# Attention and perception in one kernel: a quarter of the attention products as three passes of exact parts, dx and guides by eight products, taps along whole padded rows

## The chip, the cores and the metric

The kernel runs on one core of a Trainium2 chip. A core has a matrix engine (TensorE, in the profile PE, with its weight loads listed as PEld), a vector engine (VectorE, DVE), an activation engine (ScalarE, ACT), a general engine (GpSimd, POOL) and SyncE (SP), which here only issues DMAs. Each engine works through its own queue in order, and waits on semaphores for the others. Matrix products go from SBUF into PSUM, which has eight banks of 512 fp32 columns. The metric is the device time of one execution in microseconds, the median of the runs. The kernel before takes 3396.79 us (three runs, 3394.53 to 3397.17).

## The reference

Two layers work on a tensor of 4 images of 64 x 64 pixels with 256 channels, in fp32.

Layer 0 is full self-attention over the 4096 pixels of an image:

```python
q = x @ Wq + bq
k = x @ Wk + bk
v = x @ Wv + bv
energy = jnp.einsum('bnd,bmd->bnm', q, k)      # d = 32
attn = jax.nn.softmax(energy, axis=-1)
x_out = jnp.einsum('bnm,bmc->bnc', attn, v)
out = gamma * x_out.reshape(B, H, W, Cin) + inputs
```

Layer 1 takes its result: a depthwise 3 x 3 convolution with three outputs per channel ("perceived", 768 channels), a 1 x 1 layer to 512 channels with an exact gelu ("hidden"), a 1 x 1 layer back to 256 channels (dx) which is added to the pixels, and then an attention of each pixel over its 3 x 3 neighbours:

```python
scores = stack([(q * kp[:, 1+dy:1+dy+Hh, 1+dx:1+dx+Ww, :]).sum(-1) for dy, dx in _POS]) * scale
w = softmax(scores, axis=-1)
out = sum of w[..., i:i+1] * vp[:, 1+dy:1+dy+Hh, 1+dx:1+dx+Ww, :]
```

## The kernel before

Channels lie on partitions. The 16384 pixels are taken in 32 blocks of 512 (eight rows), eight to an image, and the program walks through 32 slots. In slot s the attention of block s is computed, the convolution of block s - 2 (`perceive`), and hidden layer, dx, guide and scores of block s - 3 (`k`), and the local products of block s - 5 (`a`). Everything is written out in order by hand, so a queue's order is the program's.

A slot has 16 points, one for each half group of 256 keys (`G`, `half`). At a point the program issues, in this order: loads for later groups; the energies (a matmul of keys and queries in the single-pass fp32 form, `float32r`) and the exponentials of them on ACT (`weight`) for two points ahead; the point's jobs (`jobs[point]`); the half group's product (`product`, L352: weights times values into two accumulators); the sum of the next half group's weights on DVE (`add_up`, L366); and then so many DVE steps of the convolution as `share` says for this point (L1152). A step is one tap (L505: window times a weight, added to the accumulator) or one of four mixes per output triple (L511). The first tap of an output is done by ACT (L501).

Ordinary fp32 matmuls appear as two instructions, those in `float32r` form as one.

The hidden layer uses Strassen's scheme in Winograd's form, seven half-size products and additions for eight products (`hidden_part`, L610 and L617). So do dx (`update_part`, with `seven`, `gather` and `update_mix`) and guides (`guide_part`, `guide_mix`): guides stand for q and k of the local attention in one, h times Wq Wk'. Their products are collected by DVE additions (L574, L576) and a few ACT copies.

At the end of a slot DVE folds the weights' sums and sums them over 32 x 32 squares (`partial_sums`, L386 and L387), a small matmul adds them over partitions (dps, L405), DVE inverts the result and spreads it (`finish`, L408, L394, L397), multiplies the accumulators by it (L417) and adds them to the pixels in the ring `xp` (L423). PE's order is: dps, then energies and point 0's jobs of the next slot, then its first product, which needs the accumulators free.

POOL works on the local attention's masks (L989) and denominators (`local_sum`, L1012). In slots 7, 15 and 23 the next image's projections of q, k and v are made as well, two or three at every second point (`projections`), and kept in DRAM; keys and values come back from there by DMAs on SP's queue (`load_keys`, `load_values`).

## Time and profile before

| | |
|---|---|
| median of 3 runs | 3396.79 us |
| profiled execution, its own time | 3395.35 us |
| its span | 3393.6 us |
| PE busy, products L352 | 3364.7 us (99%), 1833.3 us |
| DVE busy, taps L505 | 2747.1 us (81%), 1108.1 us |
| ACT busy | 1074.8 us (32%) |
| POOL busy | 352.1 us (10%) |
| DMA | 285 MB, 84 GB/s |
| granted clock of PE | 0.998 |

The busy time of an engine is the union of its instructions; the page's groups give, after the count, the busy time in us and the mean time of one in ns, and the idle time in front of them. Matmuls overlap, so the time that a series of them needs is read from the starts, not from the single durations. The page's slices show DVE at eight tenths from slot 2 on, with hardly a change from slot to slot; most slots take 99.5 us, the first ones less, and those with projections 136 us. In the views of one stretch each line has start and duration in us, engine, line, operation, the tiles (written <- read) and the number of instructions merged, and in brackets the idle time before and what ended it.

### The profile page before, as it was taken

Reading aid. Unit: us, or ns where it says so; the run is one execution under the profiler, and the core shown is the slowest. Engines: PE = TensorE matmul, PEld = TensorE weight load, DVE = VectorE, ACT = ScalarE, POOL = GpSimd, SP = SyncE. Lnnn points to the kernel's source line nnn. Section 1 sums busy time; section 2 is a strip of 40 time slices with the busy share of each in tenths; the row PEclk is TensorE's granted clock in tenths of the full one; section 3 lists DMA queues with packets and bytes.
Section 4 is the critical chain, followed back from the end, with each engine's and each line's share of the span. In section 5 each row is a group of like instructions: output and inputs, shape, how many; then the busy total and the mean of one; then the engine's idle time right before and its main releaser. Section 6 shows DMA issues by size and latency. Waiting matters only on the chain.

```text
span 3393.6 us, 32830 instructions
## 1 busy us (share of the span) xinstructions
PE 3364.7 (99%) x11678; PEld 2118.8 (62%) x11678; DVE 2747.1 (81%) x4455; ACT 1074.8 (32%) x1344; POOL 352.1 (10%) x550
## 2 busy tenths in 40 slices
PE   8999999999999999999999999999999999999998
PEld 5556666666666666666666666666666666666655
DVE  2388888867888888876888888887688888988895
ACT  2233333333332333332333323333333333333331
POOL 3000011100111110110001111101110011110031
PEclk9999999999999999999999999999999999999999
DMA  5332222342222222234222222223422222222200
GB/s 170 104 104 65 73 77 78 97 133 89 77 77 81 82 75 71 77 102 140 77 78 78 75 82 83 67 79 107 141 80 68 78 77 70 87 84 66 71 13 26
DMA packets 166126, 285.17 MB, mean 84 GB/s; under 512 B 67284, under 2 KB 68196, under 8 KB 165828
## 3 DMA queue, kind: packets, MB, share of 16 engines
q1 hardware_dynamic: 155684, 263.36, 25.1%
q10 hardware_dynamic: 9696, 17.11, 1.3%
q0 software_dynamic: 576, 2.53, 0.2%
q8 instruction: 95, 1.56, 0.2%
q14 instruction: 75, 0.61, 0.1%
HBM read 240.23 MB, written 41.94 MB: 83 GB/s over the span
## 4 chain that ended last, share of the span: by engine, by line
PE 90%; DVE 7%; DMA 2%; SPq 0%; issue 0%; ACT 0%; ACTq 0%; DVEq 0%; POOL 0%
PE acc L352 47%; PE e L333 7%; PE hid_bc L610 5%; PE hid_de L610 4%; PE hid_gf L610 4%; PE lv L923 3%; DVE perc L505 3%; PE lo L1057 3%; PE v L303 2%; PE hid_a L610 2%; DMA ka<-packed 2%; PE s L964 2%; PE dx_cd L562 1%; PE dx_ab L562 1%; PE dx_eg L562 1%; DVE den L366 1%
## 5 line engine op out<-in xcount | busy, mean ns | idle before, releaser
L352 PE MATMUL acc<-p,v 128*128 128x512 f32 x4096 | 1833.3, 593 | 0.6 <-DVE o L417 0.6
L352 PEld LDWEIGHTS acc<-p,v 128*128 128x128 f32 x4096 | 770.4, 190 | 794.7 <-issue 775.4
L505 DVE SCALAR_TENSOR_TENSOR perc<-xp,wperc,perc 128x512 f32<-128x512 f32 (+2 forms) x1554 | 1108.1, 775 | 27.6 <-ACT perc L501 27.5
L341 ACT ACTIVATE p<-e 128x1024 f32<-128x1024 f32 x512 | 524.8, 1025 | 1676.9 <-PE e L333 758.3
L366 DVE TENSOR_TENSOR den<-den,p 128x1024 f32<-128x1024 f32 x480 | 585.3, 1219 | 74.0 <-ACT p L341 72.2
L333 PE MATMUL e<-qa,ka 128*128 128x512 f32 x1024 | 364.9, 478 | 14.9 <-DMA ka<-packed 8.1
L989 POOL TENSOR_TENSOR lp<-lp,near 128x396 f32<-128x396 f32 x60 | 89.1, 1486 | 2427.8 <-ACT lp L984 2427.8
L333 PEld LDWEIGHTS e<-qa,ka 128*128 128x128 f32 x1024 | 190.5, 190 | 143.8 <-issue 101.8
L610 PE MATMUL hid_de<-perc,wmix 128*128 128x256 f32 x720 | 165.2, 379 | 0.0
L610 PEld LDWEIGHTS hid_de<-perc,wmix 128*128 128x128 f32 x720 | 136.8, 190 | 43.7 <-issue 21.5
L511 DVE TENSOR_TENSOR perc<-perc 128x256 f32<-128x256 f32 x360 | 149.9, 430 | 8.2
L633 ACT ACTIVATE hid<-hid,bup 128x512 f32<-128x512 f32 x120 | 80.4, 717 | 220.0 <-DVE hid L617 220.0
L501 ACT ACTIVATE perc<-xp,bperc,wperc 128x512 f32<-128x512 f32 x192 | 145.9, 809 | 1.7 <-DVE xp L423 1.7
L1012 POOL TENSOR_TENSOR lsum<-lsum,lp 128x99 f32<-128x99 f32 (+1 forms) x179 | 123.7, 698 | 11.7
L923 PE MATMUL lv<-wlv,h 128*128 128x256 f32 x520 | 122.4, 379 | 0.0
L303 PE MATMUL v<-wv,xc 128*128 128x256 f32 x512 | 117.9, 383 | 0.6 <-DMA wv<-in_w_v 0.5
L303 PEld LDWEIGHTS v<-wv,xc 128*128 128x128 f32 x512 | 98.1, 192 | 28.7 <-issue 15.4
L1057 PEld LDWEIGHTS lo<-lp,lv 128*128 128x128 f32 x732 | 104.9, 191 | 17.5 <-issue 9.8
L923 PEld LDWEIGHTS lv<-wlv,h 128*128 128x128 f32 x520 | 98.7, 190 | 15.5 <-issue 2.2
L1057 PE MATMUL lo<-lp,lv 128*128 128x99 f32 (+1 forms) x732 | 104.7, 291 | 0.0
L617 DVE TENSOR_TENSOR hid<-hid_bc,hid 128x512 f32<-128x512 f32 x60 | 41.5, 692 | 75.4 <-PE hid_bc L610 75.4
L341 ACT ACT_TABLE_LOAD x60 | 77.0, 1283 | 76.2 <-PE e L333 75.0
(205 smaller groups left out, 3128.6 us busy)
## 6 DMA issues: line engine op xcount, KB each, us to landing
v<-packed_v SPq DMA_DIRECT2D x248, 512.0 KB
ka<-packed SPq DMA_DIRECT2D x508, 128.0 KB
xp<-in_x SPq DMA_DIRECT2D x30, 528.0 KB
xc<-in_x SPq DMA_DIRECT2D x56, 256.0 KB
out<-lo SPq DMA_DIRECT2D x56, 256.0 KB
packed_v<-vs ACTq DMA_DIRECT2D x48, 256.0 KB
packed<-st SPq DMA_DIRECT2D x16, 512.0 KB
qa<-packed SPq DMA_DIRECT2D x62, 128.0 KB
```

The source lines that it names most:

```text
L303: nc.tensor.matmul(ps[:, i * C : (i + 1) * C], lhsT=xc[:, kin, bass.ts(2 * pair + i, P)], rhs=wv[:, kin, :], start=(kin == 0), stop=(kin = ...
L333: nc.tensor.matmul(e[:, j, :], lhsT=key[:, bass.ts(j, P)].bitcast(F32R), rhs=queries[s].bitcast(F32R), start=True, stop=True,)
L341: nc.scalar.activation(p, energies[s, G][:, 2 * half : 2 * half + 2, :], AF.Exp)
L352: nc.tensor.matmul(accs[s][c], lhsT=v[:, 2 * half + i, bass.ts(c, P)], rhs=p[:, i, :], start=(first and i == 0), stop=(G == NG - 1 and hal ...
L366: nc.vector.tensor_tensor(den, den, p, ALU.add)
L501: nc.scalar.activation(acc, win, AF.Identity, bias=bperc[:, half, j : j + 1], scale=wt)
L505: nc.vector.scalar_tensor_tensor(acc, win, wt, acc, ALU.mult, ALU.add)
L511: nc.vector.tensor_tensor(t[:, to, :], t[:, a, :], t[:, b, :], op)
L610: nc.tensor.matmul(ps[:, n * C : (n + 1) * C], lhsT=w(j), rhs=mixes[s, j][:, kind, :], start=(j == 0), stop=(j == MULT - 1),)
L923: nc.tensor.matmul(ps[:, half * C : (half + 1) * C], lhsT=keys_of(s, t, half, kin), rhs=wlv[:, kin, :], start=(kin == 0), stop=(kin == CH ...
L1012: nc.gpsimd.tensor_tensor(to, to, near_ws[block, half][:, t_, of, :], ALU.add)
L1057: nc.tensor.matmul(pv[:, rows, columns(half)], lhsT=lvs[block, t, half][:, bass.ts(c, P)], rhs=near_ws[block, half][:, t, of, :], start=(i ...
```

## The change

- In slots 1 to 30 four of the 16 half groups (2, 6, 10 and 14: `IN_PARTS`) are no longer multiplied as fp32. ACT makes a rounded "high" part of the weights (`ph`) right after the exponential, DVE a difference `low` and a combination `gap` = high - 4096 low in `add_up`, one point ahead of their use. The values have been split in the same way when they were projected, and lie in DRAM as three forms (`packed_f`). `product` then makes three passes in the single-pass form: values' high part times high, second form times low (into the same accumulators), third times gap into two further accumulators. `finish` scales these on ACT and adds them on DVE.
- The other values are stored scaled by 4096/4097, and gamma carries the inverse.
- Energies are made for one half group at a time, two banks instead of four; the accumulators take four banks instead of two. Keys have two buffers instead of three. The forms are loaded three points ahead (`load_forms`).
- dx and guides use `update` and `guide` (which the last slots used already): eight full products, two banks each, instead of seven of half the width; `seven`, `gather`, `update_mix`, `update_part`, `guide_mix`, `guide_part` and the mixed weights are gone. The jobs move over the points accordingly.
- For blocks up to 29 a tap runs over the padded rows as one run of 8 x 66 - 2 = 526 elements, instead of 8 windows of 64. The mixes take 262 elements for 256, and the hidden layer's products read 64 of every 66 columns.
- `share` has the same sum of 60 steps, laid over the points in another way.

```diff
+SPLIT = 4096.0
+BELOW = 1.0 - 2.0**-13
+IN_PARTS = (2, 6, 10, 14)
...
+            split = 2 * (s % NBLK) + pair in IN_PARTS
+            if not split or s < NBLK or s >= NSLOT - NBLK:
...
+                nc.scalar.activation(v, of, AF.Identity, scale=SPLIT / (SPLIT + 1.0))
...
+            if split:
+                whole, high, low = (fresh(f"v{n}_{s}_{pair}") for n in "whl")
+                nc.scalar.copy(whole, of)
+                nc.scalar.activation(high.bitcast(F32R), of, AF.Identity, scale=BELOW)
+                nc.vector.tensor_tensor(low, whole, high, ALU.subtract)
+                gap = fresh(f"vg_{s}_{pair}")
+                nc.vector.scalar_tensor_tensor(gap, low, -SPLIT, high, ALU.mult, ALU.add)
+                nc.scalar.mul(low, low, SPLIT)
+                for i, part in enumerate((high, low, gap)):
+                    nc.scalar.dma_start(
+                        out=packed_f[:, 2 * s + pair, i], in_=part.rearrange("p t c -> p (t c)")
+                    )
...
-            e = epsum.tile([P, GRP, NB], F32, tag="e", name=f"e_{s}_{G}", bufs=1)
+            e = epsum.tile([P, 2, NB], F32, tag="e", name=f"e_{s}_{G}_{half}", bufs=1)
...
+            if in_parts(s, G, half):
+                high = tile_of([P, 2, NB], "late", f"ph_{s}_{G}_{half}", 4)
+                nc.scalar.activation(high.bitcast(F32R), p, AF.Identity, scale=BELOW)
+                highs[s, G, half] = high
...
+            for part, (w, to, x) in enumerate((
+                (v, 0, highs[s, G, half]), (f[:, :2], 0, lows[s, G, half]), (f[:, 2:], CH, gaps[s, G, half])
+            )):
+                for i in range(2):
+                    for c in range(CH):
+                        nc.tensor.matmul(
+                            accs[s][to + c], lhsT=w[:, i, bass.ts(c, P)].bitcast(F32R),
+                            rhs=x[:, i, :].bitcast(F32R),
...
             nc.vector.tensor_tensor(den, den, p, ALU.add)
+            if in_parts(s, G, half):
+                high = highs[s, G, half]
+                low, gap = (tile_of([P, 2, NB], "late", f"p{n}_{s}_{G}_{half}", 4) for n in "lg")
+                nc.vector.tensor_tensor(low.bitcast(F32R), p, high, ALU.subtract)
+                nc.vector.scalar_tensor_tensor(
+                    gap.bitcast(F32R), low, -SPLIT, high, ALU.mult, ALU.add
+                )
...
+            for o, gap in zip(os, acc[CH:]):
+                nc.scalar.mul(o, gap, -1.0 / (SPLIT + 1.0))
...
+                    if 0 < s < NSLOT - 1:
+                        nc.vector.tensor_tensor(o, acc[c], o, ALU.add)
...
+                if s < NSLOT - LAG_PERC:
+                    acc = percs[s][i][:, :RUN]
+                    win = xp[:, half, bass.ds((at + dy) * WP + dx, RUN)]
...
-                job(local_product, a, 0), job(local_product, a, 1) + job(update_mix, k),
-                job(update_part, k, "ab"), job(update_part, k, "cd") + job(update_part, k, "eg"),
-                job(update_part, k, "f"),
-                job(guide_part, k, "ab") + job(local_values, k, 0) + job(guide_part, k, "cd"),
-                job(guide_part, k, "eg") + job(guide_part, k, "f"), job(scores, k, 0),
-                job(scores, k, 1) + job(local_sum, k - 1), job(border_terms, k), job(border, k), [],
+                job(local_product, a, 0), job(local_product, a, 1),
+                job(update, k, 0), job(update, k, 1), job(guide, k, 0),
+                job(guide, k, 1), job(local_values, k, 0), job(scores, k, 0),
+                job(scores, k, 1) + job(local_sum, k - 1), [], job(border, k), [],
...
-            share = [6, 7, 7, 5, 4, 3, 3, 3, 2, 2, 4, 5, 5, 4, 0, 0]
+            share = [0, 0, 6, 5, 5, 0, 5, 4, 4, 2, 7, 7, 7, 3, 5, 0]
...
+                soon = slot + (point + 3) // points, *divmod((point + 3) % points, 2)
+                if in_parts(*soon):
+                    load_forms(*soon)
```

## The prediction

> **What bounds the kernel now.** I read the page's engine line and chain first, then the stretch of one ordinary slot, then the vector queue at the end of that slot.

> ```profile
> PE 3364.7 (99%) x11678; PEld 2118.8 (62%) x11678; DVE 2747.1 (81%) x4455; ACT 1074.8 (32%) x1344; POOL 352.1 (10%) x550
> ...
> PE 90%; DVE 7%; DMA 2%; SPq 0%; issue 0%; ACT 0%; ACTq 0%; DVEq 0%; POOL 0%
> ```

> The stretch (window, its length, then busy time and count of PE, PEld, DVE, ACT and POOL, granted clock, DMA share, GB/s), and DVE's timeline at its end:

> ```profile
> 1713.00:1813.00 100.00, 100.00 (x350) 63.70 (x350) 86.91 (x141) 31.71 (x39) 10.12 (x15) 1.00 0.24 77
> ```

> ```profile
> 1789.81 2.73 DVE L505 SCALAR_TENSOR_TENSOR perc<-xp,wperc,perc 128x512 f32<-128x512 f32 x4
> 1792.46 1.22 DVE L366 TENSOR_TENSOR den<-den,p 128x1024 f32<-128x1024 f32 x1
> 1793.59 4.09 DVE L505 SCALAR_TENSOR_TENSOR perc<-xp,wperc,perc 128x512 f32<-128x512 f32 x5
> 1797.61 1.21 DVE L366 TENSOR_TENSOR den<-den,p 128x1024 f32<-128x1024 f32 x1
> 1798.74 4.63 DVE L505 SCALAR_TENSOR_TENSOR perc<-xp,wperc,perc 128x512 f32<-128x512 f32 x5
> 1803.30 0.34 DVE L895 TENSOR_SCALAR edge<-h,small 128x8 f32<-128x8 f32 x1
> ...
> 1805.80 1.71 DVE L511 TENSOR_TENSOR perc<-perc 128x256 f32<-128x256 f32 x4
> 1807.42 1.22 DVE L366 TENSOR_TENSOR den<-den,p 128x1024 f32<-128x1024 f32 x1
> 1808.68 0.69 DVE L368 TENSOR_TENSOR den<-den 128x512 f32<-128x512 f32 x1
> 1809.40 0.71 DVE L386 STREAM_TRANSPOSE turned<-den 128x512 f32<-128x512 f32 x1
> ...
> 1811.49 0.69 DVE L387 TENSOR_REDUCE parts<-turned 128x16 f32<-128x512 f32 x1
> 1812.94 0.36 DVE L408 RECIPROCAL inverse<-dps 128x32 f32<-128x32 f32 x1 [0.77 <-PE dps L405]
> ```

> TensorE (PE) bounds it: 99% busy, 90% of the chain. But a slot of 99.5 us holds 86.9 us of VectorE (DVE) work, and at its end both meet: the sums of the weights end at 1812.18, and the small matmul dps that needs them runs at 1812.6, when the last product is through. DVE has half a microsecond in hand there, and its other idle time (some 12 us) lies earlier, where it waits for products. So I add up each engine's queue from one dps to the next; the program's order says what stands where.

> Start-to-start prices from these lines: a tap (L505) 0.663 (2.65/4) when GpSimd (POOL) is idle, 0.80 and 0.91 when it works beside; adding up the weights of a half group 1.13, 1.26 before a dependent one; a mix of taps (L511) 0.41; the fold 0.72; the four passes of the sums 2.78.

> **The change on PE.** A plain product is two instructions per matmul (4096 in the page for 2048), spaced 0.429: 8 make 3.43 us per half group. An energy, already in the single-pass form, is one instruction; four took 0.93 (from the end of a product at 1731.90 to 1732.83). Three passes of four such matmuls cost between 12 x 0.190 (the weight load's row) and 12 x 0.2325: 2.3 to 2.8; I take 2.7, since little of the 0.93 can be a switch. That removes 0.73, four times a slot: -2.9. dx becomes 8 x 2 instructions of half the former count and twice their width: 16 x 0.429 = 6.86 for 28 x 0.216 = 6.05; the guides 8 x 0.429 = 3.43 for 14 x 0.216 = 3.02: +1.2. Energies by pairs may pay a switch twice: 0.465 to 0.50 a pair, taken 0.48, +0.2 a slot. Strided right sides of 64 in 66 columns: no row; 0, as the reads of guides in 32s cost 0.216 like the rest. PE alone would need 98.0 for 99.5.

> **The change on DVE.** Gone with the seven-product forms: 22 additions and mixes of a slot, 10.5 us by their rows (L574 4.1, L576 2.0, L697 to L716 2.8, L834 and L861 1.6). Added: in four points of 16 a difference (as L366: 1.22 with a dependent behind it) and a scale-and-subtract of 1024 elements (no row; L1070, 512 elements with a constant, takes 0.69 as the plain add does, so 1.14, bounds 1.13 and 1.3): 9.4; two additions in finish, 1.4. Each tap has 526 elements for 512: by the step from 448 to 512 elements (0.596 to 0.662) that is +0.014: 0.678, 0.7 a slot. What whole rows may save is the slowdown beside POOL: of 33 taps wholly under the masks' POOL multiply (L989) the median took 1.44 us for 0.747, while 28 contiguous adds (L366) took 1.22, as ever; but ten contiguous mixes under L1012 took 0.585 for 0.425. The bounds are 0 and all of the present 2.7 a slot; L366 is the nearest, being long and contiguous, and I take 0.5. In sum DVE's work hardly grows.

> What decides is where it stands. The new `share` puts no taps in points 0, 1 and 5, where DVE now idles behind PE, and 29 of 60 steps in points 10 to 14, where PE is shortest. Behind the local values of point 10, for which DVE must wait, the queue is: their two adds 0.76; four weight sums 4.52 and one of 1.26; difference and gap of point 14, 2.36; 21 taps 14.2; 8 mixes 3.3; fold 0.72; sums 2.78: 29.9 us. PE in the same stretch: products 2.7, 3.43, 3.43, 3.43, 2.7, 3.43, five pairs of energies 2.4, two scores 2.8, the border 0.1: 24.5. Its dps then waits 5 to 6 us (part of it already in point 14, whose low pass waits for DVE's difference).

> The slot: points 0 to 5 took 46.6 (dps 1713.10 to the energies of point 6 at 1759.66); pairs +0.1, point 2's product -0.7: 45.9. Points 6 to 9: 0.48 each, dx 2 x 3.43, guides 2 x 1.72, products 2.7 and 3 x 3.43; point 10 to its local values 0.48 + 1.73: 27.4. Then 0.27 handing over (1718.13 to 1718.40 for hid_bc), 29.9, and 0.34 to the next dps: **103.8 against 99.5, +4.3**, and 0.5 beside POOL.

> PE's wait has a price of its own, in these three rows (columns as above):

> ```profile
> 50.00:53.50 3.50, 3.50 (x17) 2.81 (x15) 0.00 (x0) 0.59 (x1) 0.00 (x0) 1.00 0.17 61
> 53.50:57.00 3.50, 1.18 (x4) 0.94 (x4) 0.00 (x0) 0.59 (x1) 0.00 (x0) 0.87 0.44 168
> 57.00:60.00 3.00, 3.00 (x6) 1.54 (x6) 1.11 (x1) 1.02 (x1) 0.00 (x0) 0.59 0.13 51
> ```

> After 2.3 us without a matmul the clock was granted at 0.59 over 3 us: about 1.7 us of work lost. A wait of 5 us every slot can bring that each time, or fall with the low clock inside itself. Bounds 0 and 3.4 (two such stretches); I take half of 1.7, 0.85, as some of it passes in the wait. [...]

> **The sum**, against the profiled execution (3395.35 us with a span of 3393.6; the median of the runs is 1.4 more). 23 full slots (5, 6, 8 to 14, 16 to 22, 24 to 30) x 5.65: +130. Slot 4 the same, +6. Slot 3, without local products, +4. Slot 2 is nothing but taps beside products: DVE 37.4 taps and mixes + 18.5 weight sums + 9.4 + 1.4 sums + 5.9 finish + 0.9 round trip = 73.5 for 66.3, and the clock: +8. Slot 1, no taps: 4 x -0.73 and pairs: -2.5. Slots 7, 15, 23, 136 us with the next image's projections, have PE enough to hide DVE: -1.5 each by PE, and about as much back for ACT, which now waits inside a projection for two DVE operations: 0. Slot 0, the same splits, +2. Slot 31 and the tail keep their work: 0. Together +148; **3395 + 148 + 1 = 3544 us**.

> Hidden and costed at nothing: the 64 MB of forms (120 loads of 512 KB on SP's queue, at a 25% DMA share; each issued three points, 10 us or more, ahead, waiting for a product already past; keys queue behind them, with three points of lead too); ACT's 4.3 us of high parts and 1.2 of scaled gaps in a 32% engine. If a key came late, PE would wait as it did for 8.1 us in all on ka. The accumulators are free 4 us after dps (two chained additions more than before), while PE has 6 us of hidden layer and values first.

> **Rivals.**
> - *Taps at contiguous speed* (ends faster). If 526 elements in a row ran at 0.45 or less, the 21 taps would give back 4.8 us, the tail would fit under PE, and each slot would be PE's 98.0: 25 x -1.5, slots 7, 15, 23 -4.5, slots 1 and 2 -5, +2: 3350. Against it: L576, all contiguous with a per-partition scalar, takes 0.39 to 0.40 for 256, as L726 on strided rows does. 0.12.
> - *POOL slows whole rows as it did windows*: 2.2 more in 24 slots, 3597. The mixes' 0.585 speak for it, L366 against. 0.20. [...]
> - *ACT held by the splits*: 16 splits, each holding the exponentials for 5 us (DVE's queue, then a write of the buffer reused): up to +64 on mine, 3608. ACT idles two thirds, the weights are two points ahead. 0.07.

> **How the numbers follow.** Mine 0.58, centre 3544; its own range 3490 (differences 1.13, pairs 0.465, no clock and no POOL loss: +3.2 a slot) to 3610 (gap 1.3, clock 1.7). With the rivals on the slow side 0.85; 0.12 for faster; the rest, 0.03, split. The range 3450 to 3620 leaves out the fast rival and the ends. A change under 0.2%, about what the runs' spread of 0.08% lets one tell, would need the tail to shrink by just 4.5 us: 0.02.

> **What would show it.** Right: DVE over 88 us busy in a slot of about 104 to 106; PE's share falling to 94-96%; waits of PE on DVE parts (dps) of 3 to 5 us in some 25 slots, and of the low pass in point 14; a granted clock under 1 after them; taps at 0.76 each by duration, also beside POOL. Wrong: taps under 0.55, or dps idle under 1 us, or the longest waits in slots 7, 15 and 23.

## The result: slower, and by twice as much as forecast

The changed kernel takes 3695.31 us (median of four runs, 3688.88 to 3705.93), the kernel before 3395.66 (four runs, 3392.83 to 3397.17): a ratio of 1.0887, with a 95% interval of 1.0856 to 1.0917. The forecast was slower, with 0.85, at 3544 us; its range ended at 3620. The sign was right, the size was not: +300 us instead of +148.

The page of the changed kernel, engines and then the chain that ended last:

```profile
PE 3452.9 (93%) x11654; PEld 2188.3 (59%) x11654; DVE 2830.6 (77%) x4172; ACT 1268.8 (34%) x1564; POOL 359.8 (10%) x542
...
PE 68%; DVE 25%; DMA 4%; issue 1%; ACT 1%; SPq 0%; ACTq 0%; DVEq 0%; POOL 0%
```

PE's share of the span fell from 99% to 93%, and a quarter of the chain is now DVE's. What PE waited for, in us in total, times, and the longest:

```profile
PE acc L410 <- DVE pl L429: 88.1, 27, 3.5
PE dps L472 <- DVE parts L454: 64.2, 26, 3.0
PE e L375 <- ACT p L380: 42.5, 12, 7.9
PE e L375 <- DMA ka<-packed: 19.6, 9, 4.9
```

The first two lines are the two waits of nearly every full slot: the low pass of point 14 waits for DVE's difference, and dps for the sums. The third is another matter: twelve waits of up to 7.9 us for an exponential; by stretches, 20.0 us of them lie in slot 23, 6.1 each in slots 7 and 15, and 10.3 in the first 300 us. That the longest waits lie in slot 23 is one of the signs that the prediction named for being wrong. Measured from one dps to the next in the two profiled executions, the 304 us between the spans (3698.0 and 3393.6) lie here:

| slots | before | after | difference | forecast |
|---|---|---|---|---|
| 20 ordinary (5, 6, 9 to 14, 17 to 22, 25 to 30), mean of one | 99.74 | 108.15 | 20 x 8.41 = +168 | 20 x 5.65 = +113 |
| 8, 16, 24, sum | 301.3 | 348.1 | +47 | +17 |
| 7, 15, 23, sum | 408.4 | 456.8 | +48 | 0 |
| 0 to 4, sum | 441.9 | 479.8 | +38 | +17.5 |
| 31 | 133.8 | 137.1 | +3 | 0 |

DVE's timeline at the end of slot 12 (start, duration), from the local values of point 10 on:

```profile
1351.62 0.76 DVE L887 TENSOR_TENSOR lv<-lv,blv 128x256 f32<-128x256 f32 x2 [2.61 <-PE lv L874]
...
1360.32 4.16 DVE L585 SCALAR_TENSOR_TENSOR perc<-xp,wperc,perc 128x526 f32<-128x526 f32 x5
1364.41 1.21 DVE L425 TENSOR_TENSOR den<-den,p 128x1024 f32<-128x1024 f32 x1
1365.54 5.95 DVE L585 SCALAR_TENSOR_TENSOR perc<-xp,wperc,perc 128x526 f32<-128x526 f32 x7
...
1383.51 0.69 DVE L454 TENSOR_REDUCE parts<-turned 128x16 f32<-128x512 f32 x1
1384.70 0.36 DVE L475 RECIPROCAL inverse<-dps 128x32 f32<-128x32 f32 x1 [0.50 <-PE dps L472]
```

DVE waits for PE once, for the local values, and then runs without a gap until dps (PE's own timeline has it at 1384.25, after a wait of 2.05). The seven taps start 0.84 us apart (1365.54 to 1371.41), the five ahead of them 0.82. So the mechanism forecast for the ordinary slot is there, and PE's waits too (3.54 us for the low pass and 2.05 for dps in this slot, for 5 to 6 forecast); the queue is 32.6 us long (1351.62 to 1384.20) instead of 29.9 and 0.5.

Ordinary slots do not all take the same time. They stand near 106.2, 107.7 and 109.2, and the difference lies in the first microseconds after dps. These windows hold 8 us from dps on, in slots 12, 13 and 14 (length, busy time and count of PE, PEld, DVE, ACT, POOL, then the granted clock, DMA share, GB/s):

```profile
1278.04:1286.04 8.00, 8.00 (x34) 6.38 (x35) 7.39 (x15) 2.34 (x3) 0.97 (x3) 1.00 0.18 62
1384.25:1392.25 8.00, 8.00 (x30) 6.75 (x31) 6.22 (x12) 2.34 (x3) 0.97 (x3) 0.79 0.17 54
1491.96:1499.96 8.00, 8.00 (x24) 6.61 (x25) 5.53 (x11) 2.45 (x3) 0.67 (x2) 0.60 0.05 19
```

PE is busy throughout, but gets 34, 30 and 24 matmul instructions done, at a clock of 1.00, 0.79 and 0.60. The clock records of the run have 311 us at half clock in all, nearly all in pieces of 3.41 us or whole multiples of it (before: 18 us). Such a piece is called a low piece below. Of the 20 ordinary slots four have none in the 60 us after dps (106.1 to 106.3), six have one of 3.4 us (107.7 to 108.0) and ten about two (109.0 to 109.3): 1.5 us for each.

And the long waits in slot 23. ACT's timeline:

```profile
2558.88 0.63 ACT L349 ACTIVATE vl<-vl 128x512 f32<-128x512 f32 x1 [2.10 <-DVE vg L348]
2558.94 0.33 ACTq L351 DMA_DIRECT2D packed_f<-vh  x1
...
2565.41 0.60 ACT L337 ACTIVATE vs<-v 128x512 f32<-128x512 f32 x1 [5.90 <-DMA packed_f<-vh]
...
2567.68 1.02 ACT L380 ACTIVATE p<-e 128x1024 f32<-128x1024 f32 x1
```

and PE's:

```profile
2558.47 3.62 PE L398 MATMUL acc<-p,v 128*128 128x512 f32 x8
2568.76 1.22 PE L375 MATMUL e<-qa,ka 128*128 128x512 f32 x2 [6.67 <-ACT p L380]
```

The copy of the second pair's values (L337) needs a buffer of `vs`, of which there are three; a split fills them with whole, high and low parts (and takes the first one again for the gap). So ACT stands for 5.9 us until the write of the high part has landed, with the exponential behind it, and PE, whose next energies need the one pair of banks free, waits for that exponential.

### The profile page after: what moved, and what is told of

The parts are those of the page before. It is cut to its first block, busy times and chain, and to the rows that moved or that the text cites. A ratio compares the mean times of both kernels' runs of the same rounds, so it can differ in the third digit from the quotient of the medians.

```text
span 3698.0 us, 33571 instructions
## 1 busy us (share of the span) xinstructions
PE 3452.9 (93%) x11654; PEld 2188.3 (59%) x11654; DVE 2830.6 (77%) x4172; ACT 1268.8 (34%) x1564; POOL 359.8 (10%) x542
## 4 chain that ended last, share of the span: by engine, by line
PE 68%; DVE 25%; DMA 4%; issue 1%; ACT 1%; SPq 0%; ACTq 0%; DVEq 0%; POOL 0%
PE acc L398 24%; DVE perc L585 12%; PE dx L711 6%; PE hid_bc L654 5%; PE e L375 5%; PE acc L410 5%; DVE den L425 4%; PE hid_gf L654 4%; PE hid_de L654 4%; PE lv L874 3%; DVE perc L591 3%; PE g L807 3%; PE hid_a L654 3%; PE lo L1008 3%; PE v L323 2%
## 5 line engine op out<-in xcount | busy, mean ns | idle before, releaser
L398 PE MATMUL acc<-p,v 128*128 128x512 f32 x3136 | 1425.0, 597 | 0.0
L585 DVE SCALAR_TENSOR_TENSOR perc<-xp,wperc,perc 128x526 f32<-128x526 f32 (+3 forms) x1554 | 1122.1, 784 | 0.7 <-ACT perc L581 0.6
L398 PEld LDWEIGHTS acc<-p,v 128*128 128x128 f32 x3136 | 597.3, 192 | 628.1 <-issue 613.1
L410 PE MATMUL acc<-pl,vf 128*128 128x512 f32 x480 | 151.1, 442 | 88.1 <-DVE pl L429 88.1
L711 PE MATMUL dx<-hid,wup 128*128 128x512 f32 x512 | 229.8, 592 | 0.0
L591 DVE TENSOR_TENSOR perc<-perc 128x262 f32<-128x262 f32 x360 | 167.5, 479 | 8.3
L410 PE MATMUL acc<-ph,v 128*128 128x512 f32 x480 | 155.5, 445 | 0.0
L430 DVE SCALAR_TENSOR_TENSOR pg<-pl,ph 128x1024 fp32r<-128x1024 f32 x120 | 148.9, 1241 | 4.1
L581 ACT ACTIVATE perc<-xp,bperc,wperc 128x526 f32<-128x526 f32 (+1 forms) x192 | 147.8, 821 | 1.7 <-DVE xp L496 1.7
L410 PE MATMUL acc<-pg,vf 128*128 128x512 f32 x480 | 146.6, 432 | 0.3
```

Source lines behind the costliest of these rows:

```text
L398: nc.tensor.matmul(accs[s][c], lhsT=v[:, i, bass.ts(c, P)], rhs=p[:, i, :], start=(first and i == 0), stop=(last and i == 1),)
L410: nc.tensor.matmul(accs[s][to + c], lhsT=w[:, i, bass.ts(c, P)].bitcast(F32R), rhs=x[:, i, :].bitcast(F32R), start=(to > 0 and n == 0 and ...
L430: nc.vector.scalar_tensor_tensor(gap.bitcast(F32R), low, -SPLIT, high, ALU.mult, ALU.add)
L581: nc.scalar.activation(acc, win, AF.Identity, bias=bperc[:, half, j : j + 1], scale=wt)
L585: nc.vector.scalar_tensor_tensor(acc, win, wt, acc, ALU.mult, ALU.add)
L591: nc.vector.tensor_tensor(t[:, to, :], t[:, a, :], t[:, b, :], op)
```

## The experiments

Four suspects: the order of DVE's steps, POOL beside whole rows, the clock, and ACT held by the splits. Each is taken away alone, then the ones that count together.

**The order alone.**

```diff
-            share = [0, 0, 6, 5, 5, 0, 5, 4, 4, 2, 7, 7, 7, 3, 5, 0]
+            share = [6, 7, 7, 5, 4, 3, 3, 3, 2, 2, 4, 5, 5, 4, 0, 0]
```

> The changed kernel with the share of the kernel before, [6, 7, 7, 5, 4, 3, 3, 3, 2, 2, 4, 5, 5, 4, 0, 0]: the order of the DVE steps alone is undone. If the loss of ordinary slots is DVE's order (steps missing from points 0, 1 and 5 and standing behind the local values of point 10) and the clock lost in the waits that follow from it, a slot falls from 108.2 us to 99 to 101: 150 to 210 us less than 3695, so 3485 to 3545, with less than 100 us at half clock in place of 311. If instead the products in three passes, dx and guides are longer on PE than I took them (98.0 a slot), the order does not matter and it stays within 1% of 3695.

Measured: 3496.37 us (3494.46 to 3500.32), ratio to before 1.0305 (1.0286 to 1.0323). The same instructions in another order take 199 us less. The window of slot 12 and PE's waits for DVE:

```profile
1220.24:1320.17 99.93, 98.36 (x344) 62.61 (x344) 88.50 (x128) 37.46 (x45) 12.01 (x15) 1.00 0.31 98
```

```profile
PE dps L472 <- DVE parts L454: 35.1, 24, 1.6
...
PE acc L410 <- DVE pl L429: 7.8, 2, 6.0
```

The ordinary slots take 99.81 on the mean, DVE has as much to do (88.5 us for 88.3), PE 98.4, and 97 us are at half clock. Still 101 us over before: 30 in slots 0 to 4, 39 in 7, 15, 23, 29 in 8, 16, 24, and 0.07 in each ordinary one. The ordinary slots' loss is the order with what follows from it; most of the rest has another cause.

**Without the splits of images 1 to 3.**

```diff
-            split = 2 * (s % NBLK) + pair in IN_PARTS
-            if not split or s < NBLK or s >= NSLOT - NBLK:
+            split = s < NBLK and 2 * s + pair in IN_PARTS
+            if True:
...
-                    of = packed_f[:, at + half, 0]
+                    of = packed_f[:, at % (2 * NBLK) + half, 0]
...
-                in_=packed_f[:, 2 * block(s, G) + half, 1:3],
+                in_=packed_f[:, 2 * G + half, 1:3],
```

> The changed kernel without the splits of the values of images 1 to 3: their blocks are projected as before (one copy, one write) and the three passes read the forms of image 0, so the same loads and products run, on other values; the splits of 12 blocks are left out. If ACT, held by the splits (buffers of vs that wait for their writes), makes slots 7, 15, 23 and 8, 16, 24 longer, those six fall to 136 to 140 and to 107 to 109: 55 to 85 us less. If those slots are longer because DVE's tail has no cover there either, or because of PE, less than 20 us go.

Measured: 3631.13 us (3604.56 to 3647.82), ratio 1.0705 (1.0629 to 1.0781): 64 us less. Windows of slots 7, 8, 23 and 24:

```profile
696.50:831.06 134.56, 134.07 (x504) 88.72 (x505) 90.35 (x132) 49.99 (x66) 13.50 (x14) 1.00 0.49 139
831.06:939.63 108.57, 100.81 (x345) 64.21 (x343) 88.42 (x128) 39.01 (x48) 9.68 (x13) 0.97 0.33 103
2478.54:2613.19 134.65, 134.07 (x505) 88.72 (x506) 90.36 (x132) 50.01 (x66) 13.43 (x14) 1.00 0.49 141
2613.19:2723.28 110.09, 101.62 (x346) 64.86 (x344) 88.50 (x128) 39.02 (x48) 9.67 (x13) 0.97 0.32 102
```

Slots 7, 15, 23 fall from 456.8 to 407.3 in sum (slot 23 from 165.2 to 134.65, with PE busy 134.07), and 8, 16, 24 from 348.1 to 327.1, which is 109.0 each, near the ordinary ones. It is the splits, not the passes, that lengthen these six. The four runs lie 43 us apart, so the 64 is rough; the profiled executions are 85 us apart, 70 of them in these six slots.

**Another buffer for the plain values.** The splits stay; what changes is what ACT waits for.

```diff
-                if s >= NBLK:
+                if s >= NBLK and s % 2:
+                    if pair == 0 or s < NSLOT - NBLK:
+                        staged[s, "v"] = tile_of([P, TPB, C], "st", f"vp_{s}")
+                    v = staged[s, "v"][:, 2 * pair : 2 * pair + 2, :]
+                elif s >= NBLK:
                     v = fresh(f"vs_{s}_{pair}")
```

> The changed kernel with another buffer for the plain values of odd blocks from 8 on: they go into the tile st, free at that time, so that the second pair no longer waits in vs for the write of the first pair's high part. Everything is still computed. If the wait for that buffer is what holds ACT in slots 7, 15, 23 and at the start of 8, 16 and 24, most of the 64 us go that leaving the splits out took away: 40 to 65 us less than 3695. If ACT is held by its second wait, for DVE's difference and gap before the scaled low part, less than 20 us go.

Measured: 3651.26 us (3635.89 to 3663.26), ratio 1.0743 (1.0705 to 1.0781): 44 us less. In the profiled execution slots 7, 15, 23 give back 38 us and 8, 16, 24 15, of the 49 and 21 without splits; the ordinary slots stand 0.45 higher, in another mixture of the steps above. The buffer is most of it. ACT's waits of the changed kernel, and then of this one:

```profile
ACT vl L349 <- DVE vg L348: 35.9, 16, 6.6
ACT vs L337 <- DMA packed_f<-vh: 29.2, 6, 5.9
ACT vs L337 <- DMA packed_f<-vg: 15.3, 3, 6.2
ACT vs L337 <- DMA packed_f<-vl: 10.6, 3, 3.9
```

```profile
ACT vl L353 <- DVE vg L352: 26.6, 16, 2.7
...
ACT vp L341 <- DMA packed_f<-vh: 3.9, 1, 3.9
```

55 us of waiting for the writes of forms have become 3.9. The wait for DVE's difference and gap stays.

**POOL taken away.**

```diff
-            if s < NSLOT - 2:
-                nc.gpsimd.tensor_tensor(pv, pv, mask, ALU.mult)
-            else:
+            if s >= NSLOT - 2:
...
-            nc.gpsimd.memset(t, 0.0)
-            for half in range(2):
-                for (block, t_), rows, of in pieces(s):
-                    to = tv[:, rows, columns(half)]
-                    nc.gpsimd.tensor_tensor(to, to, near_ws[block, half][:, t_, of, :], ALU.add)
+            nc.gpsimd.memset(t, 1.0)
```

> The changed kernel without POOL's mask multiplies and without the six additions of each local denominator (set to ones): the local attention's weights are left unmasked and unsummed in blocks up to 29. If POOL beside DVE lengthens the taps of points 11 to 13, the end of the slot, bound by DVE, comes 2.0 to 3.0 us earlier in about 25 slots: 50 to 80 us less. If the end of the slot is set by PE or by ACT, less than 15 us go.

Measured: 3639.36 us (3636.81 to 3641.38), ratio 1.0725 (1.0706 to 1.0744): 56 us less, the ordinary slot 105.66 for 108.15 (-2.5). Slots with one low piece at their start compare best: 105.1 to 105.4 here, 107.7 to 108.0 in the changed kernel, so about 2.5 for POOL. The seven taps take 4.74 us (0.68 each) for 5.87. The taps' group, of the changed kernel and without POOL's work (after the bar: busy, mean ns, idle):

```profile
L585 DVE SCALAR_TENSOR_TENSOR perc<-xp,wperc,perc 128x526 f32<-128x526 f32 (+3 forms) x1554 | 1122.1, 784 | 0.7 <-ACT perc L581 0.6
```

```profile
L585 DVE SCALAR_TENSOR_TENSOR perc<-xp,wperc,perc 128x526 f32<-128x526 f32 (+3 forms) x1554 | 1073.0, 754 | 0.7 <-ACT perc L581 0.6
```

49 us of taps in the whole kernel, and 18 of mixes (479 to 430 ns each, 360 of them), go. Whole rows are slowed beside POOL.

**Windows again.**

```diff
-        ROWS, RUN = RB // 2 * WP, RB * WP - 2
+        ROWS = RB // 2 * W
...
-                if s < NSLOT - LAG_PERC:
-                    acc = percs[s][i][:, :RUN]
-                    win = xp[:, half, bass.ds((at + dy) * WP + dx, RUN)]
-                else:
-                    acc = percs[s][i].rearrange("p (h w) -> p h w", w=W)[:, r0:r1, :]
-                    win = xv[:, half, at + dy + r0 : at + dy + r1, dx : dx + W]
+                acc = percs[s][i].rearrange("p (h w) -> p h w", w=W)[:, r0:r1, :]
+                win = xv[:, half, at + dy + r0 : at + dy + r1, dx : dx + W]
```

> The changed kernel with taps on eight windows of 64 again, mixes of 256 and hidden products on 64 of 64 columns. If whole rows are slowed beside POOL as windows are (taps of 0.82 to 0.84 us in a stretch of 1.44 or 0.84), the windows cost between 0.7 us a slot less (14 elements fewer per tap) and 0.5 more: 3675 to 3710. If whole rows do spare most of the slowdown, windows give 2 us or more a slot back to the tail: 3740 to 3760.

Measured: 3660.9 us (3658.74 to 3677.05), ratio 1.0784 (1.0765 to 1.0803): 34 us less, more than I expected of either theory, but on the side on which whole rows spare nothing. The taps' group:

```profile
L581 DVE SCALAR_TENSOR_TENSOR perc<-xp,wperc,perc 128x512 f32<-128x512 f32 (+2 forms) x1554 | 1101.6, 771 | 0.7 <-ACT perc L577 0.6
```

13 ns less per tap (771 for 784). Taken apart by what POOL does meanwhile, the medians are 0.745 and 0.759 us alone, and 1.444 (28 taps) and 1.455 (25) where a mask multiply of POOL had begun before the tap: the same slowdown for both shapes. At equal clock an ordinary slot is 0.3 us shorter (105.8 for 106.1 to 106.2 without a low piece), as the 21 taps of the tail with 14 elements less make it (21 x 0.013). The profiled executions are 23 us apart: 15 in the ordinary slots, where it is mostly the low pieces (258 us at half clock for 311, one a slot where the changed kernel has two in half of them), 8 in slots 7, 15, 23 and 3 in slot 31, less 3 in slots 0 to 4.

**The clock.** Idle matmuls where PE waits, so that it is not idle.

```diff
+        def fill(name, n):
+            ps = bank("m", name)
+            for _ in range(n):
+                nc.tensor.matmul(
+                    ps, lhsT=fold, rhs=wmix[:, 0, :2, :], start=True, stop=True
+                )
...
+                if part == 1 and n == len(IN_PARTS) - 1 and s > LAG_HID:
+                    fill(f"fill_{s}", 6)
...
+            if LAG_HID < s < NSLOT - 1:
+                fill(f"fill_dps_{s}", 5)
```

> The changed kernel with idle matmuls of PE where it waits: in slots from 4 on, six of 512 columns (2.6 us) ahead of the low pass of point 14 and five (2.1 us) ahead of dps; their results are not used. If the half clock after those waits costs up to 3.0 us a slot, as the steps of 106.2, 107.7 and 109.2 suggest, the slots settle at 106 to 106.5, under 130 us stay at half clock in place of 311, and the time falls by 30 to 55 us. If the low clock falls on work that DVE hides, it stays within 12 us, or grows where a slot had less to wait for than the filler.

Measured: 3695.02 us (3693.38 to 3698.59), ratio 1.088 (1.0862 to 1.0898): no difference, and neither theory is served by that, because I had sized the fillers wrongly. An ordinary fp32 matmul of 512 columns is two instructions, spaced 0.429 us in the trace before; five make 4.29 us. PE was busy 107.24 us of 107.24 in slot 12, so the fillers themselves were the bound. Yet the clock was 1.00 there, 91 us were at half clock in all, and the mean ordinary slot fell from 108.15 to 107.28, while slots 7, 15, 23 grew by 33 us, having little to wait for there. The run was repeated with three and two matmuls, and none in those three slots:

> The run with idle matmuls again, at half their size, and none in slots 7, 15, 23: an fp32 matmul of 512 columns is two instructions of 0.429 us, so the six and five were 5.15 and 4.29 us, longer than the waits that they were to fill, and held the ordinary slots at 107.3. Now three (2.57 us) ahead of the low pass of point 14 and two (1.72) ahead of dps. If the half clock is what lifts slots from 106.2 to 107.7 and 109.2, the ordinary ones all take 106.1 to 106.5 and the time is 30 to 50 us less than 3695. If the low clock costs nothing beyond the waits, the mean of the slots stays at 108 and the time within 10 us.

Measured: 3667.19 us (3664.6 to 3669.7), ratio 1.0805 (1.0788 to 1.0822): 28 us less, just under the 30 to 50 expected. Slots 12 and 13:

```profile
1275.20:1383.18 107.98, 104.60 (x355) 65.62 (x355) 88.52 (x128) 37.45 (x45) 11.66 (x16) 0.98 0.29 90
1383.18:1489.25 106.07, 102.89 (x354) 64.42 (x355) 88.22 (x128) 37.45 (x45) 10.08 (x15) 1.00 0.29 92
```

The step at 109.2 is gone; eight of 20 slots still have one low piece (107.7 to 108.0), twelve have none (106.1 to 106.3). 134 us are at half clock for 311, and the mean slot is 106.85: 1.30 us less with more instructions on PE and DVE's queue untouched. If all had stood at 106.1 it would have been 2.0. So the low clock costs an ordinary slot about 2 us, of its 8.4. It is the pieces at the start of a slot that cost: the four slots at 106.1 to 106.3 of the changed kernel have two low pieces each behind the wait of point 14, these twelve have none, and the time is the same.

**Without the three passes**, with the order of before:

```diff
-            return 0 < s < NSLOT - 1 and 2 * G + half in IN_PARTS
+            return False
...
-            split = 2 * (s % NBLK) + pair in IN_PARTS
+            split = False
...
-                n = 2 * CH if 0 < s < NSLOT - 1 else CH
+                n = CH
```

(the additions in `finish` and the `share` of the change are undone as well)

> The kernel with the share of before and without the products in three passes: all half groups as fp32, no splits, no forms, two accumulators. What stays of the change: dx and guides by eight products, energies in pairs, two key buffers and whole rows. Against the run with the share alone (3496): four products cost 0.73 more each, so an ordinary slot of PE work goes from 98.3 to 101.2, about 1.4 over the 99.8 measured there; slots 7, 8, 15, 16, 23, 24 lose their holds of ACT (60 to 70 us) and slots 0 to 2 theirs (20 to 30). 3430 to 3460. If the three passes themselves are the loss, it comes below 3400.

Measured: 3427.69 us (3423.72 to 3429.43), ratio 1.0092 (1.0075 to 1.0109), just under the 3430 to 3460 expected. So the rest of the change alone is 0.9% slower. The ordinary slot takes 100.61, of which PE is busy all the time, for 99.74 before: 17 us in the 20 of them, where dx and guides by eight products are the likely cause. Another 10 lie in slots 0 to 4. No run gave dx and guides their seven products back, the energies their four banks or the keys their third buffer, so these are not told apart.

**Image 0 as fp32**, in the changed kernel:

```diff
-            return 0 < s < NSLOT - 1 and 2 * G + half in IN_PARTS
+            return NBLK <= s < NSLOT - 1 and 2 * G + half in IN_PARTS
...
-            split = 2 * (s % NBLK) + pair in IN_PARTS
+            split = s >= NBLK and 2 * (s % NBLK) + pair in IN_PARTS
```

(the two further accumulators and their additions go with it)

> The changed kernel with image 0 as fp32: three passes, their differences and two further accumulators only in slots 8 to 30, no splits of blocks 0 to 7. If slot 0 is longer by ACT held in the splits, and slots 1 and 2 by DVE's differences with too little PE work beside them, these three give back 10 to 15, 3 to 4 and 3 to 5 us, as without any passes; slots 3 to 7 hardly change, since four products cost PE 2.9 more each but DVE's tail has one difference and gap less. 3660 to 3685. If it is key loads with two buffers that lengthen slots 0 and 1, less than 10 us go.

Measured: 3684.22 us (3673.35 to 3689.66), ratio 1.086 (1.0843 to 1.0877): 11 us less on the medians, at the edge of the 3660 to 3685 expected. In the profiled execution slots 0, 1 and 2 give back 16.0, 1.6 and 4.4 us, and PE's waits for exponentials in the first 300 us fall from 10.3 to 1.1; slots 3 and 4 give 1.9, and slots 7 and 15 take 5.2 more. Slot 0 is the least steady of all, but it was 133 to 138 in the eight profiled executions with splits in it and 118 to 127 in the five without. Keys from DRAM, with two buffers, still hold PE there (7.0 us, 12.0 in the changed kernel), and slot 1 stays 3.4 over before.

**What this points to.** Passes only from slot 8 on, the other buffer, windows, and a `share` with more of the steps in front, found by adding up the queues as in the prediction:

```diff
-            share = [0, 0, 6, 5, 5, 0, 5, 4, 4, 2, 7, 7, 7, 3, 5, 0]
+            share = [7, 3, 4, 7, 5, 4, 5, 3, 3, 5, 3, 7, 3, 1, 0, 0]
```

> What the runs point to: three passes only from slot 8 on (image 0, where slots 0 to 2 have too little PE work to hide the splits and DVE's differences, stays as fp32), windows for the taps, the buffer st for the plain values of odd blocks, and the share [7, 3, 4, 7, 5, 4, 5, 3, 3, 5, 3, 7, 3, 1, 0, 0], which leaves DVE some 3 us in hand at the end of a slot. If order, buffer and image 0 were the whole loss, the ordinary slots from 9 on take 98.3 to 98.7, slots 4 to 6 100.5 to 101.2, slots 7, 15, 23 134 to 137, and the time is 3365 to 3395, level with the kernel before or below it. If PE loses more in the passes than the trace of one slot shows, 3400 or more.

Measured: 3381.11 us (3379.23 to 3383.15), ratio 0.9956 (0.9939 to 0.9972): below the kernel before. The same with whole rows instead of windows:

> The version that the runs point to (3381), with taps along whole padded rows instead of windows. If whole rows cost only the elements they add, and these lie beside PE's products wherever DVE has time in hand, it comes within 6 us of 3381. If whole rows disturb more than DVE's own queue, it loses 20 us or more, as they lost 34 in the changed kernel.

Measured: 3381.4 us (3380.03 to 3385.74), ratio 0.9961 (0.9946 to 0.9976): no difference. What whole rows cost in the changed kernel (0.3 us a slot at equal clock) they cost because DVE's queue was the bound at the end of the slot; where PE is the bound, their 22 us of taps (1098.8 us for 1077.2) are hidden. Last, windows, and the end of a split held back until after the next even point's exponential:

```diff
-                nc.scalar.mul(low, low, SPLIT)
-                for i, part in enumerate((high, low, gap)):
-                    nc.scalar.dma_start(
-                        out=packed_f[:, 2 * s + pair, i], in_=part.rearrange("p t c -> p (t c)")
-                    )
+                def write():
+                    nc.scalar.mul(low, low, SPLIT)
+                    for i, part in enumerate((high, low, gap)):
+                        nc.scalar.dma_start(
+                            out=packed_f[:, 2 * s + pair, i],
+                            in_=part.rearrange("p t c -> p (t c)"),
+                        )
+
+                held.append(write)
...
                     energy(*after, half)
+                while held and half == 0:
+                    held.pop()()
```

> The version that the runs point to (3381), with the scaling of the low part and the three writes of a split held back to the start of the next even point, after that point's exponential, so that ACT never waits there for DVE's difference and gap. If that wait still lengthens slots 7, 15, 23 (137 to 138 us where the PE work left needs 134) and 8, 16, 24 (101 to 104 for 98 to 99), 8 to 20 us go: 3361 to 3373. If those slots are long for another reason (keys from DRAM, the buffers of the projections), it stays within 4 us.

Measured, in five runs: 3374.32 us (3370.87 to 3375.06), ratio 0.9941 (0.9928 to 0.9955), 7 us less than the version without it, just under the 8 to 20 expected. How much of the 7 is the edit's is open: the profiled executions are 12 us apart, 6 of them in slots 7, 8, 15, 16, 23 and 24 and 6 in slots 0 to 4, in which no split runs. ACT's waits for DVE's difference and gap (17.8 us in the version without it) are gone, so what is left in the six slots is mostly something else. Its page, and its slots 12, 23 and 24:

```profile
PE 3332.7 (99%) x11542; PEld 2093.3 (62%) x11542; DVE 2715.5 (81%) x4094; ACT 1222.1 (36%) x1510; POOL 377.0 (11%) x542
...
PE 93%; DMA 3%; DVE 2%; SPq 0%; issue 0%; ACT 0%; ACTq 0%; POOL 0%; DVEq 0%
```

```profile
1179.97:1277.75 97.78, 97.78 (x345) 62.84 (x344) 87.26 (x128) 37.36 (x45) 12.02 (x15) 1.00 0.32 99
2297.31:2433.75 136.44, 134.66 (x505) 88.35 (x504) 93.50 (x139) 55.56 (x78) 8.27 (x13) 1.00 0.54 161
2433.75:2535.39 101.64, 98.33 (x344) 62.94 (x345) 88.83 (x130) 39.41 (x49) 11.57 (x14) 1.00 0.35 110
```

The changed kernel's own passes, with DVE out of the way, make an ordinary slot 97.8 us. Slots 8, 16, 24 (304.1 in sum) and the waits for keys (15.2 us) still hold something.

## Why the prediction was right in sign and wrong in size

- *PE alone needs 98.0*: right. It is 97.78 where PE is never waiting. A product in three passes saves (100.58 - 97.78) / 4 = 0.70 us; I had 0.73. So the change's gain on PE is real, about 1.9 us a slot net.
- *DVE's sum hardly grows, its place decides*: right. 86.9 us busy before, 88.3 after. Moving the steps back, with nothing else, took 199 of the 300 us away.
- *The front of 73.3, from dps to the local values, and 0.27 to hand over*: 73.58 (dps at 1278.04, DVE on the local values at 1351.62). *The tail of 29.9, DVE's queue from there to the next dps*: 32.6. The term that failed is "I take 0.5" for POOL, with "L366 is the nearest, being long and contiguous". It was not: the 21 taps took 16.3 us for 14.2 and the 8 mixes 3.9 for 3.3, from start to start. The rival "POOL slows whole rows as it did windows" was the right reading, at +2.2; the slot without a low clock is at 106.2, 1.9 over 103.8 and 0.5. The mixes' 0.585 for 0.425, contiguous too, had spoken for it, and windows and whole rows, at 1.444 and 1.455 us where a multiply had begun first, agree with them; I should have gone by them. What spared the additions is in the trace before, here POOL and then DVE:

```profile
1792.69 1.80 POOL L989 TENSOR_TENSOR lp<-lp,near 128x396 f32<-128x396 f32 x1 [78.17 <-ACT lp L984]
```

```profile
1792.46 1.22 DVE L366 TENSOR_TENSOR den<-den,p 128x1024 f32<-128x1024 f32 x1
1793.59 1.44 DVE L505 SCALAR_TENSOR_TENSOR perc<-xp,wperc,perc 128x512 f32<-128x512 f32 x1
```

The addition began 0.23 us before the mask multiply and took its usual 1.22 us; the multiply ended 0.81 us after it; the tap behind, begun while the multiply ran, took 1.44 us for 0.747. So it is throughout this trace: 53 additions that began before a multiply took 1.22 us, and it ended 0.81 us after each; 56 taps that began second took 1.44, and 5 that began first 0.74. In the changed kernel 25 whole rows that began second took 1.455 and 53 that began first 0.758. For the taps of both shapes the time thus went with which of the two had begun first. The additions that I priced by had begun first; none of them met a multiply for more than 0.06 us that was already running, so they never showed what I took from them.

- *The clock, 0.85, bounds 0 and 3.4*: measured 0, 1.5 or 3.0 a slot, about 2.0 on the mean. The bounds held; what failed was halving the one stretch in the trace because part of it would "pass in the wait". The slot has two waits. Low pieces behind the one of point 14 do pass in the wait for dps and cost nothing; those behind dps, one or two in 16 of 20 slots, fall on work that PE is the bound of, and cost 1.5 us each.
- *Slots 7, 15 and 23 at 0, since they have PE enough to hide DVE*: the step that failed outright. PE's work does hide DVE there. What it does not hide is ACT: the splits hold the exponentials, and with the energies on one pair of banks PE stands after one point (the banks by the kernel's order; no run gave the other pair back). I had this as a rival at 0.07, worth "up to +64", with "ACT idles two thirds" against it; leaving the splits out gave 64, about as much, though 12 of the 16 splits were left out and slots 8, 16 and 24 are in it. An engine's share of idle time says nothing about an instruction that stands in its queue for 5.9 us. Of that rival, too, the mechanism was only half right: most of the holding is the buffer that waits for its write, the smaller part DVE's turn.
- *Slots 8, 16 and 24 as ordinary ones*: failed for the same reason. The last split of an image is made at the end of the slot before, and the scaling of the two gap accumulators, new on ACT, stands behind it.
- *Slot 0 at +2, slot 1 at -2.5*: +13.6 and +5.0 measured. The splits again, as far as leaving them out of image 0 shows it; and keys with two buffers, which no run undid, in slot 1. Slots 2, 3 and 4 came as forecast (+8.7, +4.1, +6.7 for +8, +4, +6), slot 4 partly by luck: it has no low piece at its start, and its forecast had 0.85 for the clock.
- *The rivals as alternatives*: this is what made the range too short. They did not exclude each other, or my own case. 3544 and the two prices that I gave, 53 for POOL and 64 for ACT, make 3661; with a clock of 2.0 for 0.85 in 23 slots (+26) and slots 0 and 1 (+19) it is 3706, for 3695 measured.
- *Taps at contiguous speed*: 0.759 us for a whole row alone. The rival is out.

## What to carry to other kernels

Before a kernel whose bound engine saves work is called faster, add up the queue of the second engine from the last point at which it must wait to the point at which the first one waits for it; the same steps in another order were worth 199 us of 3695 here. Look at each engine that is mostly idle for instructions that will stand in its queue (a buffer that is reused before its write has landed, a turn on another engine) and for what stands behind them. Before a row is taken to show that an instruction is not slowed beside another engine, see which of the two began first (a tap took 1.44 us here when it began second and 0.74 when it began first). Rivals that can hold at the same time are terms of one sum, and the range has to reach to their sum.

## What the runs showed of the hardware

```profile
1276.45:1279.86 3.41, 1.82 (x9) 1.63 (x10) 2.81 (x6) 0.83 (x1) 0.68 (x2) 1.00 0.60 177
1279.86:1283.28 3.42, 3.42 (x17) 2.99 (x17) 3.35 (x8) 1.51 (x3) 0.00 (x0) 1.00 0.08 31
1382.26:1385.67 3.41, 1.42 (x7) 1.27 (x8) 2.81 (x6) 0.43 (x1) 0.67 (x2) 1.00 0.64 175
1385.67:1389.09 3.42, 3.42 (x9) 2.70 (x8) 3.35 (x8) 1.91 (x3) 0.00 (x0) 0.50 0.08 32
```

With PE idle for 1.59 us the clock stayed at 1.00, with 1.99 the next stretch was at 0.50. Counted over the traces of all 14 kernels (behind the first 20 us, by the records of the matmuls): a stretch at full clock with PE idle for 2.1 us or more was followed by one at half clock in 286 of 286 cases, with less than 1.5 in none of 13436, in between in 84 of 187. A stretch at half clock was the last one when PE was idle in it for at most 0.2 us (306 of 306), and never when for more than 0.8 (117). So waits of 1.85, 2.05 and 2.89 us, as they lay on the grid, gave slots 12, 13 and 14 their 1.00, 0.79 and 0.60.

- Kernels that wait in every slot differed more from run to run: 3604.56 to 3647.82 without the splits of images 1 to 3, 3635.89 to 3663.26 with the other buffer, for 3370.87 to 3375.06 where PE hardly waits. In those two the mean granted clock goes with the time, 0.969 to 0.962 and 0.966 to 0.961 from the fastest run to the slowest. So the low pieces probably fell differently; only one execution of each has a trace to show where.
- Idle matmuls kept the clock up: 311 us at half clock became 134 with 3 and 2 of them a slot, and the slots got shorter by 1.3 us although PE did more.
